# First weight's sums on VectorE, late loads of bias rows and rim, and score batches of two in layer 1 of a four-layer convolution sequence

## The chip, the cores and the metric

The kernel runs on one NeuronCore of one Trainium2 chip. The metric is device time in microseconds (us) of one execution, and the number to compare is the median of several runs. The engines are named as in the profile: PE is TensorE (matmuls), PEld its weight loads, DVE is VectorE, ACT is ScalarE, POOL is GpSimd, SP is SyncE, which here only issues DMAs.

## The reference

The input `x` is float32, 8 images of 512 channels of 32 by 32 pixels (S = 1024 positions). Four layers follow one another, cut here to what matters:

```python
# layer 0: group norm, eight-head attention over positions, three tanh steps, projection, residual
h = group_norm(x); q, k, v = split(qkv_w @ h + qkv_b)
h = softmax(q.T @ k / 8) @ v                    # per head, 64 channels each
for _ in range(3): h = h + 0.1 * tanh(inl_w @ h + inl_b)
x = x + proj_w @ h + proj_b
# layer 1: one attention with 64 channels for queries and keys, 512 for values, no scaling
q, k, v = Wq @ x + bq, Wk @ x + bk, Wv @ x + bv
x = softmax(q.T @ k) applied to v + x
# layer 2: add a bias per channel, 12-tap upsampling by 2, leaky relu, 12-tap downsampling by 2
# layer 3: mixture of eight experts: 1x1, 3x3 and 1x1 convolutions whose weights are mixed per image
```

Everything is float32.

## The kernel before

**Stages.** The batch loop runs over the eight images `b`. For each it does `layer0`, `layer1` and `layer2`; layer 3 follows for all images at the end. `x_next` of the next image is loaded and its norm statistics are taken while the present image is worked on.

**Products in seven steps.** The 512 by 512 products (q, k, v, the tanh steps, the projection, and layer 1's values) are done by a Strassen-like scheme on quarters, in the generator `product`. Each `next()` issues one of its seven steps: P1 and C11 accumulate in two banks "A" of the PSUM pool `ps_mm`; U2, U3, C21 in banks "X" and C22, C12 in banks "Y" of the pool `ps_sc`. The steps need sums of quarters of both operands: `quarter_sums` makes the data's sums on DVE (tiles named `T_...`, eight instructions), and for the first image `weight_sums` makes the weights' on POOL (parts 3 to 6 of the weight tile; part 2 is minus a22) and stores them in DRAM, from where later images load them. The weight tile's parts are used in the order A11 (P1), A12 (C11), S2 (U2), S3 (U3), S1 (C22), -A22 (C21), S4 (C12). P1 and C11 need no sums at all.

**Order of work.** Except where `manual_schedule` is written (layer 0's attention), a planner orders each engine's instructions: it follows program order where it can and takes a later instruction that is ready, by its own estimate, when an earlier one is not. All engines execute their own queue in order. A tile from a pool with n buffers waits until the n-th tile before it is released.

**Start.** SP issues the loads of `x` of image 0, of the quarters of the q, k and v weights, and of the q and k weights of layer 1 (`w_qk`). POOL issues the small constants, the bias rows `v_row`, `row_bias`, `bias2` (each broadcast to 128 partitions), and four writes of a zero tile `rim0` to the rims of the two DRAM scratch images `ypad`. DVE takes the statistics (L286), the norm factors (L295 to L308), then makes `h` (L314, four instructions of 128x1024) and the sums of `h`. POOL makes the sums of the q weights (L362 to L366), then those of k and v. The argument `held` of `weight_sums` puts a one-element copy ahead, into the sum's own place, so that the sums of k and v start only after the sums of `h`.

**Layer 1.** `quarter_sums` of `x`; a projection with 128 columns for q and k together (`qk`, L322) into the two banks of the pool `ps_tp`, copied out by DVE and ACT; then the steps of the value product and the scores are interleaved. `scores(t)` does one of eight tiles: two matmuls (r = 0 and 1) that use 64 rows of the array each and so run beside each other (L271), two banks for the results, from `ps_tp` where t is even and from `ps_mm` where it is odd, and two exponentials on ACT (L767). `totals(0)` sums the exponentials of the first half over the partitions with four one-column matmuls (L782) into one bank of `ps_tp`, and DVE takes the reciprocal (L786). Each of the two pools has two banks. After the last step the transposes of `x` (L808) and the product of the weights with the values (L905) follow. The order is given by

```python
        for _ in range(2):
            next(values)
        for steps in ((0,), (1, 2), (3, 4), (5, 6), (7,)):
            for t in steps:
                scores(t)
            next(values)
            if 4 in steps:
                totals(0)
```

**A second copy.** If a bound is exceeded the whole sequence would be run again with `shifted=True`; that copy is in the program and isn't run on these inputs.

Of the kernel before, what the change touches and what calls it, by code (L numbers as in the profile page):

```python
# [17 lines left out]
P = 128  # L18
B, C, H, W = 8, 512, 32, 32
S = H * W  # L20
# [33 lines left out]
def tile_sequence(ctx: ExitStack, tc: tile.TileContext, a: dict, out: bass.AP, shifted: bool):  # L54
# [12 lines left out]
    def big_tile(name, shape):  # L67
        return big.tile(shape, F32, tag="big", name=name)
# [5 lines left out]
    def tmp(name, n=HALF):  # L74
        if n == HALF:
            return work.tile([P, n], F32, tag="half", name=name, bufs=2)
        return work.tile([P, n], F32, tag="tmp", name=name, bufs=6)
# [37 lines left out]
    nc.vector.memset(seen_sums, 0.0)  # L115

    v_row = const.tile([P, C], F32, name="v_row")
    nc.gpsimd.dma_start(v_row, a["v_b"].partition_broadcast(P))
    qk1_b = const.tile([P, 1], F32, name="qk1_b")
    nc.gpsimd.dma_start(qk1_b[0:HD, :], a["bq"])  # L120
    nc.gpsimd.dma_start(qk1_b[HD:P, :], a["bk"])
# [1 line left out]

    row_bias = const.tile([P, C], F32, name="row_bias")
    bias2 = tmp("bias2")
    nc.gpsimd.dma_start(row_bias, a["bv"].partition_broadcast(P))
    nc.gpsimd.dma_start(bias2, a["bias"].partition_broadcast(P))
    nc.vector.tensor_add(row_bias, row_bias, bias2)

    up_op = const.tile([P, UR * UC], F32, name="up_op")  # L130
    up_left_op = const.tile([P, UR * UC], F32, name="up_left_op")
# [106 lines left out]


    rim0 = tmp("rim0")  # L240
    nc.vector.memset(rim0, 0.0)
    for t in ypad:
        nc.gpsimd.dma_start(t[0 : 3 * W], rim0[0 : 3 * W])
        nc.gpsimd.dma_start(t[(H + 3) * W :], rim0[0 : 2 * W])


    pooled = const.tile([P, CC, B], F32, name="pooled")
# [63 lines left out]
    def group_norm(b, x, mul, add):  # L311
        h = big_tile(f"h_{b}", [P, CC, S])
        for cc in range(CC):
            nc.vector.tensor_scalar(  # L314
                h[:, cc, :], x[:, cc, :], mul[:, cc : cc + 1], add[:, cc : cc + 1],
                ALU.mult, ALU.add,
            )
        return h
# [19 lines left out]
    def weight(key, b):  # L338
        if not b:
            return weight_sums(key, *weight_quarters(key, tmp(f"raw_{key}", S)))  # L340
        t = wpool.tile([P, len(PARTS), 2, QR], F32, tag="w", name=f"w_{key}_{b}", bufs=3)
        nc.sync.dma_start(t, stored[key])
        return t
# [14 lines left out]
    def weight_sums(key, t, a21, a22, held=None):  # L358
        if held is not None:

            nc.gpsimd.tensor_copy(t[:, 3, 0, 0:1], held)
        nc.gpsimd.tensor_add(t[:, 3], a21, a22)  # L362
        nc.gpsimd.tensor_sub(t[:, 4], t[:, 3], t[:, 0])
        nc.gpsimd.tensor_sub(t[:, 5], t[:, 0], a21)
        nc.gpsimd.tensor_sub(t[:, 6], t[:, 1], t[:, 4])
        nc.gpsimd.tensor_scalar(t[:, 2], a22, -1.0, None, ALU.mult)  # L366
        nc.gpsimd.dma_start(stored[key], t)
        return t

    def quarter_sums(name, src, ccs=(0, 1), into=None):  # L370


        t = into
        if t is None:
            made = big_tile(f"T_{name}", [P, 8, HALF])
            at = ((0, 1), (7, 2), (6, 3), (5, 4))
            t = [[made[:, i, :] for i in pair] for pair in at]
        for cc in ccs:
            b11, b12 = src[:, cc, 0:HALF], src[:, cc, HALF:S]
            b21, b22 = src[:, cc + 2, 0:HALF], src[:, cc + 2, HALF:S]  # L380
            nc.vector.tensor_sub(t[0][cc], b12, b11)
            nc.vector.tensor_sub(t[1][cc], b22, t[0][cc])
            nc.vector.tensor_sub(t[2][cc], b22, b12)
            nc.vector.tensor_sub(t[3][cc], t[1][cc], b21)
        return t
# [39 lines left out]
    def all_of(gen):  # L425
        for _ in gen:
            pass
# [140 lines left out]

    def layer0(b, x, norm, w):
        h = group_norm(b, x, *norm)  # L570
        t = quarter_sums(f"h_{b}", h)
        if b == 0:
            for key in "kv":
                w[key] = weight_sums(key, *held[key], t[3][1][:, 0:1])
        q = big_tile(f"q_{b}", [P, CC, S])
        k = big_tile(f"k_{b}", [P, CC, S])
        v = big_tile(f"v_{b}", [P, SC, C])
        all_of(product(f"q_{b}", w["q"], h, t, channels(f"q_{b}", q, qkv_b[:, 0:CC])))
        w["inl"] = weight("inl", b)
        all_of(product(f"k_{b}", w["k"], h, t, channels(f"k_{b}", k, qkv_b[:, CC : 2 * CC])))  # L580
        w["proj"] = weight("proj", b)
# [22 lines left out]
        def scores(t):  # L604
            g, jc = divmod(t, SC)
            oc, sh = groups[g]
            pair = ps_sc.tile([P, S], F32, tag="scores", name=f"scores_{b}_{t}")
            ps = [pair[:, ts(r, HALF)] for r in range(2)]
            for r in range(2):
                for c in range(2):  # L610
                    nc.tensor.matmul(  # L611
                        ps[r][rows[c]],
                        k[rows[r], oc, jc * P + c * HD : jc * P + c * HD + HD],
                        q[rows[r], oc, ts(sh, HALF)],
                        start=True, stop=(shifts is None),
                    )
            if shifts is not None:
                for r in range(2):
                    nc.tensor.matmul(
                        ps[r], ones[HD * r : HD * r + 1, :],  # L620
                        shifts[HD * r : HD * r + 1, oc, ts(sh, HALF)],
                        start=False, stop=True, skip_group_check=True,
                    )
            e = tmp(f"e_{b}_{t}", S)
            nc.scalar.activation(e, pair, AF.Exp, scale=HD ** -0.5)  # L625
            exps[t] = e
            if jc == 1:
                accs[g] = sums(f"acc_{b}_{g}")
                nc.vector.tensor_add(accs[g], exps[t - 1], e)  # L629
            elif 1 < jc < SC - 1:  # L630
                nc.vector.tensor_add(accs[g], accs[g], e)  # L631
            elif jc == SC - 1:
                nc.vector.scalar_tensor_tensor(
                    accs[g], accs[g], 1.0, e, ALU.mult, ALU.add,
                    accum_out=seen_sums[:, b, g : g + 1],
                )
# [84 lines left out]
    def layer1(b, x, w, midway):  # L721
# [3 lines left out]

        rows = [slice(HD * r, HD * r + HD) for r in range(2)]
        t_x = quarter_sums(f"x_{b}", x)
        for sh in range(2):
            ps = bank(ps_tp, name=f"qk1_{b}_{sh}")
            project(ps, w["qk1"], 0, x, sh)  # L730
            keys = ps[HD:P, :].rearrange("d (p r j) -> d p r j", r=2, j=P)
            for r in range(2):
                dst = k[rows[r], 2 * sh : 2 * sh + 2, :]
                if r == 0:
                    nc.vector.tensor_scalar_add(q[rows[r], ts(sh, HALF)], ps[0:HD, :], qk1_b[0:HD, :])
                    nc.vector.tensor_scalar_add(dst, keys[:, :, r, :], qk1_b[HD:P, :])
                else:
                    nc.scalar.activation(
                        q[rows[r], ts(sh, HALF)], ps[0:HD, :], AF.Identity, bias=qk1_b[0:HD, :]
                    )  # L740
                    nc.scalar.activation(
                        dst, keys[:, :, r, :], AF.Identity, bias=qk1_b[HD:P, :]
                    )
        shift = None
        if shifted:
# [3 lines left out]
                [qk[rows[r], S : S + HALF] for r in range(2)],  # L749
                [shift[HD * r : HD * r + 1, :] for r in range(2)],  # L750
            )
        v = big_tile(f"v1_{b}", [P, SC, C])
        eT = [big_tile(f"eT_{b}_{sh}", [P, SC, HALF]) for sh in range(2)]
        inv = small.tile([P, SC], F32, tag="inv1", bufs=2, name=f"inv1_{b}")
        accs = {}
# [31 lines left out]
            nc.gpsimd.tensor_add(seen, seen, both)  # L787
            nc.gpsimd.tensor_add(seen[:, 0:4], seen[:, 0:4], inv[:, at])

        values = product(f"v1_{b}", w["v1"], x, t_x, positions(f"v1_{b}", v), rows=True)  # L790
        for _ in range(2):
            next(values)
        for steps in ((0,), (1, 2), (3, 4), (5, 6), (7,)):
            for t in steps:
                scores(t)
            next(values)
            if 4 in steps:
                totals(0)
        all_of(values)
        if b + 1 < B:  # L800
# [235 lines left out]
        return z  # L1036

    with tc.tile_pool(name=f"weights_{run}", bufs=1) as wpool:
        w = {"q": weight("q", 0)}
        raw = big_tile("raw_kv", [P, 2, S])  # L1040
        held = {key: weight_quarters(key, raw[:, i, :]) for i, key in enumerate("kv")}
        w["qk1"] = wpool.tile([P, CC, P], F32, name="w_qk1")
        for i, key in enumerate(("q1_wT", "k1_wT")):
            nc.sync.dma_start(
                w["qk1"][:, :, ts(i, HD)], a[key].rearrange("(cc p) o -> p cc o", p=P)
            )

        norm = norm_factors(0, channel_stats(0, x_next))
        for b in range(B):
            x, last = x_next, b + 1 == B  # L1050
            layer0(b, x, norm, w)
            if not last:
                x_next = load_x(b + 1)
            stats = []

            def midway():
                if not last:
                    stats.append(channel_stats(b + 1, x_next))

            halo = layer1(b, x, w, midway)  # L1060
            if not last:
                norm = norm_factors(b + 1, *stats)
                layer2(b, halo)
# [239 lines left out]
```

## Time and profile before

Three runs gave 3828.47, 3828.78 and 3829.96 us; the median is 3828.78 us. The execution that was profiled took 3826.37 us, of which 3824.6 us are the span from the first to the last instruction.

| | before |
|---|---|
| median of three runs | 3828.78 us |
| profiled execution, its span | 3826.37 us, 3824.6 us |
| mean granted TensorE clock | 0.997 |
| PE busy | 3764.8 us (98%) |
| DVE busy | 2572.6 us (67%) |
| ACT busy | 1202.9 us (31%) |
| POOL busy | 100.3 us (3%) |
| DMA | 248.67 MB, mean 65 GB/s |

In the timeline a row is: start in us, busy time in us, engine, line, operation, what it writes and reads, shape, count of instructions; in brackets, where the engine sat idle before it, how long and what ended that. A float32 matmul shows as two matmul records. In the chain of waits a row is start, length, and what the end of the kernel waited for in that stretch.

### The profile page before, as it was taken

The page shows a single profiled execution, that of the slowest core. Times are in us where ns is not written, and L with a number is a line of the kernel's source. Part 1 is how long each engine was busy: PE and PEld are TensorE (multiplying, and loading weights), DVE is VectorE, ACT ScalarE, POOL GpSimd, SP SyncE. Part 2 cuts the span into 40 slices and gives each one's busy share as a digit, 9 for nine tenths or more (in the row PEclk, how much of TensorE's full clock was granted, in tenths as well). Part 3 has the DMA queues.
Part 4 walks back from the last instruction along what each step waited for, and adds up shares of the span by engine and source line. Part 5 has one row for each costly group of instructions (what it writes and reads, how often), then busy time and mean ns, then how long its engine had stood idle before and what let it go on. Part 6 is the DMA issues. An engine that isn't in the chain of part 4 may idle for free.

```text
span 3824.6 us, 50438 instructions
## 1 busy us (share of the span) xinstructions
PE 3764.8 (98%) x20838; PEld 1996.0 (52%) x20838; DVE 2572.6 (67%) x3887; ACT 1202.9 (31%) x1707; POOL 100.3 (3%) x118
## 2 busy tenths in 40 slices
PE   8999999999999999999999999999999999999999
PEld 4346653475435753466534754357534754347543
DVE  5877948664686648775586647765487656866885
ACT  0631226212442116312252124422162123521333
POOL 5000000000000000000000000000000000001000
PEclk9999999999999999999999999999999999999999
DMA  5002310123101310023101220023201131003432
GB/s 199 24 1 86 115 63 1 42 76 106 39 1 61 121 70 11 1 85 119 58 1 61 84 92 27 1 80 102 80 1 42 52 129 41 1 1 124 161 145 98
DMA packets 85841, 248.67 MB, mean 65 GB/s; under 512 B 10480, under 2 KB 33024, under 8 KB 78816
## 3 DMA queue, kind: packets, MB, share of 16 engines
q1 hardware_dynamic: 69712, 220.23, 16.2%
q10 hardware_dynamic: 13824, 12.59, 1.0%
q0 software_dynamic: 2064, 12.51, 0.9%
q8 instruction: 166, 2.72, 0.3%
q14 instruction: 75, 0.61, 0.1%
HBM read 185.40 MB, written 59.90 MB: 64 GB/s over the span
## 4 chain that ended last, share of the span: by engine, by line
PE 93%; DVE 4%; ACT 1%; DMA 1%; issue 0%; SPq 0%; ACTq 0%; DVEq 0%
PE scores L611 12%; PE av L647 12%; PE inl_X L417 6%; PE dn L995 5%; PE v_X L417 4%; PE inl_A L417 4%; PE inl_Y L417 4%; PE up L971 4%; PE av_X L905 3%; PE c L1209 3%; PE v_Y L417 3%; PE av_A L905 3%; PE av_Y L905 2%; PE v_A L417 2%; PE proj_X L417 2%; PE q_X L417 2%
## 5 line engine op out<-in xcount | busy, mean ns | idle before, releaser
L625 ACT ACTIVATE e<-scores 128x1024 f32<-128x1024 f32 x512 | 523.2, 1024 | 673.5 <-PE scores L611 624.8
L611 PE MATMUL scores<-q,k 64*64 64x512 f32 x4096 | 535.8, 593 | 3.6 <-DVE v L498 3.6
L647 PE MATMUL av<-e,v 64*64 64x512 f32 x4096 | 531.0, 589 | 0.0
L631 DVE TENSOR_TENSOR acc<-acc,e 128x1024 f32<-128x1024 f32 x320 | 389.5, 1217 | 38.5 <-ACT e L625 36.5
L611 PEld LDWEIGHTS scores<-q,k 64*64 64x64 f32 x4096 | 153.8, 133 | 297.6 <-issue 208.5
L647 PEld LDWEIGHTS av<-e,v 64*64 64x64 f32 x4096 | 161.3, 133 | 278.2 <-issue 275.2
L417 PE MATMUL inl_X<-T_hf,w_inl 128*128 128x512 f32 x576 | 262.9, 592 | 0.0
L955 DVE SCALAR_TENSOR_TENSOR up<-up,leak 128x512 f32<-128x512 f32 x264 | 173.5, 688 | 115.3 <-ACT leak L954 110.0
L954 ACT ACTIVATE leak<-up 128x512 f32<-128x512 f32 x264 | 149.5, 596 | 249.5 <-DVE up L955 127.7
L668 DVE RECIPROCAL inv<-av 128x256 f32<-128x256 f32 x128 | 223.0, 1747 | 0.0
L995 PEld LDWEIGHTS dn<-dn_op,up 128*64 128x64 f32 (+1 forms) x4096 | 193.2, 136 | 56.5 <-issue 28.8
L995 PE MATMUL dn<-dn_op,up 128*64 128x126 f32 (+5 forms) x4096 | 210.5, 255 | 8.8 <-DVE up L955 7.9
L971 PE MATMUL up<-halo,up_op 126*128 126x512 f32 (+1 forms) x384 | 183.7, 611 | 0.8 <-DVE up L955 0.6
L417 PEld LDWEIGHTS inl_X<-T_hf,w_inl 128*128 128x128 f32 x576 | 108.7, 190 | 138.6 <-issue 105.8
L417 PE MATMUL inl_A<-hf,w_inl 128*128 128x512 f32 x384 | 172.2, 594 | 0.0
L511 ACT ACTIVATE inl_U<-inl_U,inl_b 128x512 f32<-128x512 f32 x96 | 66.7, 718 | 307.6 <-DVE inl_U L526 307.6
L629 DVE TENSOR_TENSOR acc<-e,e 128x1024 f32<-128x1024 f32 x64 | 78.8, 1232 | 112.0 <-ACT e L625 112.0
L522 DVE TENSOR_TENSOR inl_U<-inl_X,inl_P 128x512 f32<-128x512 f32 x96 | 61.9, 687 | 121.7 <-PE inl_X L417 118.9
L1209 PE MATMUL c<-rim,mixed 128*128 128x512 f32 x288 | 124.9, 592 | 0.0
L417 PEld LDWEIGHTS inl_A<-hf,w_inl 128*128 128x128 f32 x384 | 72.2, 190 | 94.6 <-issue 90.4
L905 PE MATMUL av_X<-v,eT 128*128 128x256 f32 x512 | 118.8, 380 | 1.8 <-DVE av_W L884 1.0
L905 PE MATMUL av_A<-v,eT 128*128 128x256 f32 x512 | 119.1, 381 | 0.0
(304 smaller groups left out, 5561.1 us busy)
## 6 DMA issues: line engine op xcount, KB each, us to landing
halo<-ypad_u SPq DMA_DIRECT2D x128, 252.0 KB
halo<-ypad_u SPq DMA_DIRECT2D x128, 198.0 KB
w_v<-stored_u_v SPq DMA_DIRECT2D x14, 1792.0 KB
x<-in_x_dram SPq DMA_DIRECT2D x32, 512.0 KB
spill_u<-z SPq DMA_DIRECT2D x28, 512.0 KB
z<-spill_u SPq DMA_DIRECT2D x28, 512.0 KB
out_dram<-z SPq DMA_DIRECT2D x28, 512.0 KB
w_q<-stored_u_q SPq DMA_DIRECT2D x7, 1792.0 KB
```

Of the source, the lines that this page charges most:

```text
L417: nc.tensor.matmul(dst, lhs, rhs, start=(opens and s == 0 and cc == 0), stop=(cc == 1 and s == rows), skip_group_check=True,)
L611: nc.tensor.matmul(ps[r][rows[c]], k[rows[r], oc, jc * P + c * HD : jc * P + c * HD + HD], q[rows[r], oc, ts(sh, HALF)], start=True, stop= ...
L625: nc.scalar.activation(e, pair, AF.Exp, scale=HD ** -0.5)
L631: nc.vector.tensor_add(accs[g], accs[g], e)
L647: nc.tensor.matmul(avs[g][r][rows[c]], v[rows[r], jc, ts(2 * oc + c, HD)], e[rows[r], ts(c, HALF)], start=(jc == 0), stop=(jc == SC - 1),)
L668: nc.vector.reciprocal(copies[g][:, at], totals[g][:, at])
L905: nc.tensor.matmul(ps[:, ts(s, QR)], left[:, j, at : at + P], right[:, j, :], start=(what in ("P1", "U2", "W") and s == 0 and j == 0), sto ...
L954: nc.scalar.mul(t, ps, 0.2 * SQRT2)
L955: nc.vector.scalar_tensor_tensor(dst, ps, SQRT2, t, ALU.mult, ALU.max)
L971: nc.tensor.matmul(ps[i], op[0 : IR * n, :], halo.tile(t)[0 : IR * n, c + i, :], start=True, stop=True,)
L995: nc.tensor.matmul(rows[part, r0 - first : r1 + 1 - first, c0 : c1 + 1], up[t][0:k, c, ts(2 * cc + s, HD)], op[:, r0 - 4 * t + 3 : r1 + 4 ...
L1209: nc.tensor.matmul(banks[g].rearrange("p (h w) -> p h w", w=W), wt[:, at : at + P], h1[:, ky + 16 * g : ky + 16 * g + 16, kx : kx + W], st ...
```

## The change

The sums of the first weight (q, image 0) are made on DVE by `first_sums` and `first_rest`, one of them (part 2) on ACT, instead of by `weight_sums` on POOL: two of them before the sums of `h`, two after. `first_sums` is held until the last quarter of `h` is written. The sums of k and v stay on POOL, where now three one-element copies each, instead of one, hold them back. The loads of `v_row`, `row_bias` and `bias2` and the four writes of the rim move from POOL's queue to SP's, behind the loads of all first weights; the zero tile is set by POOL instead of DVE; the addition of `bias2` to `row_bias` moves behind image 0's q product.

In layer 1 the first step of the value product (P1) comes ahead of the projection of q and k, and the scores come in four batches of two behind three steps, instead of in batches of one, two, two, two, one behind two steps. `totals(0)` comes after the batch of t = 4 and 5 and step C21; before, it came after t = 3 and 4 and step C22.

In the copy with `shifted=True` the added term of layer 0's scores is done by four matmuls instead of two.

```diff
-    nc.gpsimd.dma_start(v_row, a["v_b"].partition_broadcast(P))
...
-    nc.gpsimd.dma_start(row_bias, a["bv"].partition_broadcast(P))
-    nc.gpsimd.dma_start(bias2, a["bias"].partition_broadcast(P))
-    nc.vector.tensor_add(row_bias, row_bias, bias2)
...
     rim0 = tmp("rim0")
-    nc.vector.memset(rim0, 0.0)
-    for t in ypad:
-        nc.gpsimd.dma_start(t[0 : 3 * W], rim0[0 : 3 * W])
-        nc.gpsimd.dma_start(t[(H + 3) * W :], rim0[0 : 2 * W])
+    nc.gpsimd.memset(rim0, 0.0)
+
+    def late_loads():
+        nc.sync.dma_start(v_row, a["v_b"].partition_broadcast(P))
+        nc.sync.dma_start(row_bias, a["bv"].partition_broadcast(P))
+        nc.sync.dma_start(bias2, a["bias"].partition_broadcast(P))
+        for t in ypad:
+            nc.sync.dma_start(t[0 : 3 * W], rim0[0 : 3 * W])
+            nc.sync.dma_start(t[(H + 3) * W :], rim0[0 : 2 * W])
...
     def weight_sums(key, t, a21, a22, held=None):
         if held is not None:
-            nc.gpsimd.tensor_copy(t[:, 3, 0, 0:1], held)
+            for i in (3, 5, 2):
+                nc.gpsimd.tensor_copy(t[:, i, 0, 0:1], held)
...
+    def first_sums(t, a21, a22, held):
+        nc.vector.tensor_copy(t[:, 3, 0, 0:1], held)
+        nc.vector.tensor_add(t[:, 3], a21, a22)
+        nc.vector.tensor_sub(t[:, 4], t[:, 3], t[:, 0])
+
+    def first_rest(t, a21, a22):
+        nc.vector.tensor_copy(t[:, 5, 0, 0:1], t[:, 4, 0, 0:1])
+        nc.vector.tensor_sub(t[:, 5], t[:, 0], a21)
+        nc.scalar.mul(t[:, 2], a22, -1.0)
+        nc.vector.tensor_sub(t[:, 6], t[:, 1], t[:, 4])
+        nc.gpsimd.dma_start(stored["q"], t)
+        return t
...
     def layer0(b, x, norm, w):
         h = group_norm(b, x, *norm)
+        if b == 0:
+            first_sums(*held["q"], h[:, CC - 1, 0:1])
         t = quarter_sums(f"h_{b}", h)
         if b == 0:
+            w["q"] = first_rest(*held["q"])
             for key in "kv":
                 w[key] = weight_sums(key, *held[key], t[3][1][:, 0:1])
...
         all_of(product(f"q_{b}", w["q"], h, t, channels(f"q_{b}", q, qkv_b[:, 0:CC])))
+        if b == 0:
+            nc.vector.tensor_add(row_bias, row_bias, bias2)
...
         t_x = quarter_sums(f"x_{b}", x)
+        v = big_tile(f"v1_{b}", [P, SC, C])
+        values = product(f"v1_{b}", w["v1"], x, t_x, positions(f"v1_{b}", v), rows=True)
+        next(values)
         for sh in range(2):
             ps = bank(ps_tp, name=f"qk1_{b}_{sh}")
             project(ps, w["qk1"], 0, x, sh)
...
         for _ in range(2):
             next(values)
-        for steps in ((0,), (1, 2), (3, 4), (5, 6), (7,)):
-            for t in steps:
+        for first in range(0, SC, 2):
+            for t in (first, first + 1):
                 scores(t)
             next(values)
-            if 4 in steps:
+            if first == 4:
                 totals(0)
...
-        w = {"q": weight("q", 0)}
+        w = {}
+        held = {"q": weight_quarters("q", tmp("raw_q", S))}
         raw = big_tile("raw_kv", [P, 2, S])
-        held = {key: weight_quarters(key, raw[:, i, :]) for i, key in enumerate("kv")}
+        for i, key in enumerate("kv"):
+            held[key] = weight_quarters(key, raw[:, i, :])
...
+        late_loads()
```

## The prediction

> **What bounds the kernel now.** The page first: busy time and the chain that ended last.
>
> ```profile
> PE 3764.8 (98%) x20838; PEld 1996.0 (52%) x20838; DVE 2572.6 (67%) x3887; ACT 1202.9 (31%) x1707; POOL 100.3 (3%) x118
> ...
> PE 93%; DVE 4%; ACT 1%; DMA 1%; issue 0%; SPq 0%; ACTq 0%; DVEq 0%
> ```
>
> PE sets the end nearly everywhere, so an edit counts only where it removes an idle PE or PE time itself. Where PE is idle I looked up in PE's waits and, in the two stages that the change touches, in the timeline. The start, all engines:
>
> ```profile
> 13.56 0.48 DVE L241 MEMSET rim<- 128x512 f32 x1
> ...
> 15.17 9.57 PE L417 MATMUL q_A<-h,w_q 128*128 128x512 f32 x16 [2.37 <-DVE h L314]
> ...
> 17.01 1.67 POOL L362 TENSOR_TENSOR w_q<-raw_q 128x512 f32<-128x512 f32 x1
> ...
> 17.48 1.75 DVE L128 TENSOR_TENSOR row_bias<-row_bias,bias 128x512 f32<-128x512 f32 x1
> ...
> 20.82 1.75 DVE L381 TENSOR_TENSOR T_h<-h 128x512 f32<-128x512 f32 x1
> ...
> 26.06 1.10 PE L417 MATMUL q_X<-T_h,w_q 128*128 128x512 f32 x2 [1.32 <-DVE T_h L382]
> ...
> 28.11 0.68 DVE L382 TENSOR_TENSOR T_h<-h,T_h 128x512 f32<-128x512 f32 x1
> ...
> 28.85 2.84 PE L417 MATMUL q_X<-T_h,w_q 128*128 128x512 f32 x6 [1.69 <-DVE T_h L382]
> ...
> 45.26 7.03 PE L417 MATMUL k_A<-h,w_k 128*128 128x512 f32 x16
> ```
>
> To be seen: DVE needs 1.75 us for a sum of two SBUF operands while POOL computes (17.01 to 26.99) and 0.68 us when POOL is not computing; PE waits twice for those sums. Layer 1 of image 0, PE alone (the other seven images show the same lengths, shifted):
>
> ```profile
> 317.68 5.34 PE L417 MATMUL v_A<-w_v,x 128*128 128x256 f32 x24
> 323.27 1.99 PE L417 MATMUL v_A<-w_v,x 128*128 128x256 f32 x8 [0.25 <-ACT v_P L481]
> 325.19 1.13 PE L271 MATMUL scores<-qk 64*128 64x512 f32 x4
> 326.25 3.72 PE L417 MATMUL v_X<-w_v,T_x 128*128 128x256 f32 x16
> 329.90 1.99 PE L271 MATMUL scores<-qk 64*128 64x512 f32 x8
> ```
>
> And where `totals(0)` stands, all engines:
>
> ```profile
> 340.94 0.95 PE L782 MATMUL total<-ones,acc 128*128 128x1 f32 x8
> ...
> 341.14 1.29 DVE L498 TENSOR_TENSOR v<-v_Y,v_U 128x512 f32<-128x512 f32 x2 [1.45 <-PE v_Y L417]
> 341.82 1.99 PE L271 MATMUL scores<-qk 64*128 64x512 f32 x8
> ...
> 342.35 0.17 DVE L786 RECIPROCAL inv<-total 128x4 f32<-128x4 f32 x1
> ```
>
> The reciprocal stands on DVE behind the two additions of the step before and ends 0.70 us after the scores have started. That costs nothing now: t = 5, whose banks are free, goes first.
>
> **Start, q's wait.** Records of q_A are 0.59 us long at a pitch of 0.43 (weight loads at 20.72, 21.15, 21.58), so the next could follow 0.16 before the row's end: 24.74 - 0.16 = 24.58. Forty records remain, 40 x 0.43 = 17.2, so k could start at 41.8; it starts at 45.26. The two waits cost 3.5 us. After the change DVE makes h (four at a pitch of 0.72, from the rows at 14.30 and 15.03 in a narrow window), S1 and S2 (0.61 pitch each), eight sums of h (4.9), S3 and S4. From h's start at 14.3 less 0.8 (below): h to 16.5, S1 and S2 to 17.8, the sixth sum of h (the last that U2 needs, as now ordered) to 21.4, all to 22.6, the rest to 23.9. PE would reach U2 at 24.58 - 0.8 = 23.8. Slack 2.4 us, so the 3.5 us go whole. What is late next is PE's own rate. The cover goes only if POOL computes beside DVE: with 1.75 us for eight of these it would be 16.5 + 8 x 1.75 = 30.5, and the gain is lost. POOL's remaining sums (k, v) are held until the last sum of h, and its rim writes leave.
>
> S3 and S4 can meet POOL's k sums: two times 1.75 from 22.6, ready at 26.1 against U3 at 23.8 + 3.4 = 27.2. The Trainium skill, "SBUF — State Buffer", "Who interferes with whom", speaks against putting them there: a VectorE instruction with two SBUF inputs and a GpSimd one that reads SBUF exclude each other for the whole instruction. By that rule each could wait out one POOL sum (1.26 us alone, in the row of w_v at 33.05) and S4 would end at 22.6 + 2 x (1.26 + 0.68) = 26.5, an estimate; the sum is the same.
>
> **Start, ahead of h.** The zero tile's memset (0.48 us) stands on DVE between two norm factors, and the last statistics waited 0.35 us for x (row at 9.19). The first goes to POOL, which has idle time there (1.29 us before 8.14). The second should go with the bias rows (256 KB each, first issued at 4.46) out of x's way: 5 to 10 us is DMA at 345 GB/s and 98% busy. About 0.8 us together; bounds 0.4 (x no earlier) and 0.9. The first records are 0.86 us apart until about 20.1, 4.9 us after the first, though the granted clock reads 1.00; I take 4.9 as a length that moves along. If the fast pitch came at a fixed time, half of the 0.8 would be lost, 0.4. The Trainium skill, "TensorE: Matmul & The Clock Gate", "Part 1", says the slow state ends with a busy window of 3.4 us on a free-running grid; by it the slow stretch would be anything from 3.4 to 6.8 us, an estimate, as much noise as gain.
>
> **Start, at nothing.** Seven more issues on SP, about 0.4 us each like w_qk's, put the inl weights' loads 3 us later (17.45 to 20.5); POOL reads them at 45.52. `v_row` is first needed at about 70, the rims at 396. The row_bias addition (0.68 to 1.75) falls into the q product, where DVE is busy 10.4 of 20 us. ACT's multiplication (about 0.6) is needed by step C21, some 10 us after U2. Two more guard copies for k and v cost POOL 4 x 0.17; k's sums end near 32, used from 48. The second copy does not run. Start in all: -3.5 - 0.8 = **-4.3 us**, once; bounds -4.5 and -3.5.
>
> **Layer 1, removed.** (a) P1 now waits on ACT behind the copies of q and k: 24 records at 0.2155 from 317.68 end at 322.85, the next starts at 323.27: 0.42 us. With P1 ahead of q and k, ACT has copied it long before C11. (b) Two batches of one take 2 x 1.06 (325.19 to 326.25), one of two 1.92 (329.90 to 331.82): 0.20 less. A value step between batches takes 3.65 (326.25 to 329.90), without them 3.45 (the chain's v_X row in layer 0): another 0.20. Sum 0.82 us an image, 8 x 0.82 = **-6.6 us**. q and k are copied out within 4.9 us of their last matmul (317.7 to 322.6); C11 and U2 cover 6.9.
>
> **Layer 1, added.** After `totals(0)` the next scores are t = 6, in the pool whose second bank holds the totals. Its second matmul must wait for the reciprocal; t = 5, which covers that now, has gone. Relative to the totals' start, scores start at 0.88 and the reciprocal ends at 1.58, whether the step before is C22 or C21 (two additions either way). A weight load follows a DVE end by about 0.06, so r = 1 starts at 1.64 instead of 0.88: 0.76 us, and r = 0 and t = 7 stand behind it in PE's queue. 8 x 0.76 = **+6.1 us**. Lower bound 0, if the planner puts t = 7 ahead whole; upper bound 0.86 (one t alone) if it splits the pair so that the halves no longer run together. I take 0.76, the row as it stands. The batch's two exponentials more at the end (2.06 instead of 1.08) lie under C12's 3.65.
>
> **Sum.** -4.3 - 6.6 + 6.1 = -4.8 us on the profiled 3826.37 (span 3824.6, 1.8 outside). The profiled run is 2.4 below the median of 3828.78; the same difference on the median gives **3824.0 us**. A measurement here can tell about 0.2%, 7.7 us, from no change, so this case is "within".
>
> **Rivals.** A: no new wait, -4.3 - 6.6 = -10.9, 3817.9. For it: the planner takes what is ready, as its two qk matmuls amid the projection show. Against: t = 6 has one free bank, so it comes first, and t = 7 then only halves a pair.
>
> B: the start doesn't gain (POOL still beside DVE, or h's quarter sums before S2): -0.8 - 6.6 + 6.1, -1.3, 3827.5. For it: the planner ordered T_h and w_q as it liked. Against: the guards.
>
> C, slower: on DVE the sums of layer 1's last product (L856, two of 0.6, running right after C21's additions at 348.70 today) get ahead of the reciprocal, and with them an addition of exponentials (1.13). The wait becomes 0.76 + 1.2 = 2.0, or 3.1: -4.3 - 6.6 + 8 x 2.0 = +5.1, 3833.9, or +13.9, 3842.7. It decides from 1.36 us of wait (10.9 / 8). Against: today the reciprocal comes right after the additions.
>
> Beside these, PE's two long waits (6.47 us at 419.69 behind DVE, followed by a clock of 0.50; 5.62 at 3524) may shift by 2 us if the planner's order does; this is in every range.
>
> **How the numbers follow.** Main case 0.58 (3820 to 3828), A 0.22 (3816 to 3820), B 0.08, C 0.12. Over 0.2% faster (below 3821.1): nine tenths of A and a sixth of the main case, 0.30. Slower (above 3836.4): the longer form of C, two thirds of it, 0.08. Within: 0.62. The range 3816 to 3832 leaves out the lower edge of A and most of C.
>
> **What would show it.** q_X without a wait after q_A and k_A near 41; sums of h at 0.68; h at 13.5. In layer 1 no wait for v_P, four score batches, and between the totals and t = 6 a wait for DVE's reciprocal of some 0.7 us, eight times. Without that wait, A; with more DVE work ahead of L786, C. A PE wait elsewhere than these makes it wrong.

## Result and profile after

The changed kernel took 3831.87 us (median of 22 runs, 3824.95 to 3846.33), the kernel before 3828.41 us on the same chip (22 runs, 3825.99 to 3831.52). The ratio is 1.0013, 95% interval 1.0008 to 1.0019: slower by 0.13% (by the two medians alone, 0.09%). That lies inside the forecast's range and within its 0.2%, but 7.9 us above the forecast, and the kernel became slower where it was to become 4.8 us faster. The profiled execution took 3831.41 us, with a span of 3829.6 us (before: 3824.6).

The page after, busy time and the chain that ended last:

```profile
PE 3773.7 (99%) x20838; PEld 2004.4 (52%) x20838; DVE 2568.8 (67%) x3892; ACT 1206.7 (32%) x1708; POOL 88.2 (2%) x111
...
PE 94%; DVE 3%; DMA 1%; ACT 1%; issue 0%; SPq 0%; ACTq 0%; DVEq 0%
```

PE is 8.9 us longer busy with the same number of instructions. So the time was lost in matmuls that took longer, or that look longer because something stands between them. The timeline of the start, all engines:

```profile
13.73 2.98 DVE L315 TENSOR_SCALAR h<-x,gmul,gadd 128x1024 f32<-128x1024 f32 x4
14.60 8.93 PE L432 MATMUL q_A<-h,w_q 128*128 128x512 f32 x16 [2.01 <-DVE h L315]
...
17.90 0.68 DVE L374 TENSOR_TENSOR w_q<-raw_q 128x512 f32<-128x512 f32 x1
...
23.37 3.60 PE L432 MATMUL q_X<-T_h,w_q 128*128 128x512 f32 x8
...
40.54 5.74 PE L432 MATMUL k_A<-h,w_k 128*128 128x512 f32 x13
```

q_X follows q_A without a wait, the sums take 0.68 us, and k starts at 40.54 instead of 45.26. The start did what was forecast; what of the 4.72 us is the change's own is worked out below. Layer 1 of image 0, PE alone:

```profile
316.31 3.62 PE L432 MATMUL v_A<-w_v,x 128*128 128x256 f32 x16
319.77 3.62 PE L432 MATMUL v_X<-w_v,T_x 128*128 128x256 f32 x16
323.31 1.99 PE L272 MATMUL scores<-qk 64*128 64x512 f32 x8
325.23 3.72 PE L432 MATMUL v_X<-w_v,T_x 128*128 128x256 f32 x16
...
339.93 0.95 PE L805 MATMUL total<-ones,acc 128*128 128x1 f32 x8
340.80 3.79 PE L272 MATMUL scores<-qk 64*128 64x512 f32 x8
344.52 2.64 PE L432 MATMUL v_Y<-w_v,x 128*128 128x256 f32 x11
```

The wait for `v_P` is gone. But the batch behind the totals takes from 340.80 to 344.52, 3.72 us, where the batch at 323.31 takes 1.92 (to 325.23) with the same eight records. No idle time of PE stands at it. The same stretch with the other engines:

```profile
340.80 0.29 PEld L272 LDWEIGHTS scores<-qk 64*128 64x128 f32 x2
...
341.33 0.17 DVE L809 RECIPROCAL inv<-total 128x4 f32<-128x4 f32 x1
...
341.96 0.60 ACT L790 ACTIVATE eT<-scores 128x512 f32<-128x512 f32 x1 [4.29 <-PE scores L272]
...
342.61 0.29 PEld L272 LDWEIGHTS scores<-qk 64*128 64x128 f32 x2 [0.66 <-ACT eT L790]
342.82 0.60 ACT L790 ACTIVATE eT<-scores 128x512 f32<-128x512 f32 x1 [0.26 <-PE scores L272]
```

The wait stands in the row of the weight load: at 342.61 it waits for ACT's first exponential, which ends at 341.96 + 0.60 = 342.56. The matmul held there is read as t = 6, r = 1: it has been given the bank that r = 0 of the same t wrote, so it can't start until that has been read (experiment 5, where it stands second in the queue, shows the same wait). Meanwhile r = 0 of t = 7, on the same half of the array as r = 0 of t = 6, fills PE, and the two r = 1 follow on the other half. Eight records then stand one behind the other (8 x 0.43 + 0.28 = 3.72) instead of in four pairs (4 x 0.43 + 0.20 = 1.92). The reciprocal, at 341.33 to 341.50, is not what it waits for. Of PE's waits the changed kernel shows none at these scores, and of the weight loads' waits exactly eight, one an image:

```profile
PEld scores L272 <- issue: 27.2, 104, 0.5
...
PEld scores L272 <- ACT eT L790: 5.3, 8, 0.7
```

(A row is: total idle in us, how often, mean in us.) In the kernel before the second row doesn't exist. In image 6 the stretch cost more. Windows from 3001 us, with PE's busy time first and the granted clock in the third column from the end:

```profile
3001.00:3008.30 7.30, 7.30 (x32) 5.14 (x31) 4.38 (x7) 2.75 (x6) 0.50 (x1) 1.00 0.00 0
3008.30:3015.20 6.90, 6.90 (x14) 4.04 (x14) 3.66 (x4) 1.30 (x3) 1.26 (x1) 0.51 0.01 2
3015.20:3022.00 6.80, 6.80 (x45) 5.98 (x44) 5.40 (x8) 0.00 (x0) 0.00 (x0) 1.00 0.66 228
```

The clock was granted at half for 6.8 us, beginning amid this batch, and the image lost another 3.33 us. Half-clock stretches are in the trace of before too (10.24 us from 416.06, 6.83 us from 3522.19), but those two begin in PE's long waits in layer 2. Here PE's records leave no gap.

### The profile page after: what moved, and what is told of

Read it like the earlier page. It is cut to its first block, busy times and chain, and to the rows that moved or that the text cites. A ratio compares the mean times of both kernels' runs of the same rounds, so it can differ in the third digit from the quotient of the medians.

```text
span 3829.6 us, 50461 instructions
## 1 busy us (share of the span) xinstructions
PE 3773.7 (99%) x20838; PEld 2004.4 (52%) x20838; DVE 2568.8 (67%) x3892; ACT 1206.7 (32%) x1708; POOL 88.2 (2%) x111
## 4 chain that ended last, share of the span: by engine, by line
PE 94%; DVE 3%; DMA 1%; ACT 1%; issue 0%; SPq 0%; ACTq 0%; DVEq 0%
PE scores L631 12%; PE av L668 11%; PE inl_X L432 6%; PE dn L1017 5%; PE v_X L432 4%; PE inl_A L432 4%; PE inl_Y L432 4%; PE up L993 4%; PE av_X L927 4%; PE c L1234 3%; PE v_Y L432 3%; PE av_A L927 3%; PE v_A L432 3%; PE av_Y L927 2%; PE q_X L432 2%; PE proj_X L432 2%
```

## Experiments

"k minus h" is the time from the first `h` to the first record of k_A. Layer 1 is compared per image, from the first scores of layer 0's attention to the first transpose (L808 before). Intervals are of the ratio to the kernel before.

**1. The start alone, layer 1 as before.**

```diff
-        for first in range(0, SC, 2):
-            for t in (first, first + 1):
+        for steps in ((0,), (1, 2), (3, 4), (5, 6), (7,)):
+            for t in steps:
...
-            if first == 4:
+            if 4 in steps:
```
(and P1 back behind q and k)

> The changed start, layer 1 as in the kernel before. Theory M (the loss is all in layer 1's last score batch, where the halves of t = 6 and t = 7 no longer run in pairs): the changed kernel's k_A starts at 40.54 instead of 45.26, so 4.7 us less than before, about 3823.7, and nothing else moves; the clock of every run stays at 0.997 as before. Rival S (the start's gain is given back later, at image 0's wait for DVE or by another clock period, so layer 1 isn't the cause): within 1.5 us of before, or slower.

Measured: 3825.23 us against 3827.94, ratio 0.9990 (0.9981 to 0.9999). A gain of 2.7 us, the forecast's 4.3 within its interval. k minus h is 27.30, before 30.96.

**2. Layer 1 alone, the start as before.** The reverse of 1.

> The start as before, layer 1 changed. Theory M: eight times 0.9 us more up to the transposes, half of that given back in the product that follows, and in some runs a period of half clock more: 4 to 12 us slower than before, with runs that spread over 10 us and clocks down to 0.993; the totals are followed by scores that take 3.7 us instead of 1.9. Rival S: layer 1 costs nothing by itself, within 2 us of before, with a narrow spread.

Measured: 3839.43 us against 3827.94, ratio 1.0028 (1.0017 to 1.0039). The loss is layer 1's. In each of the eight images the last batch takes 3.72 us. The two halves of the change don't add up: -2.7 and +11.5 make +8.8, the whole change +3.5. The runs of 2 and of the whole change spread over 8 and 21 us, with mean clocks of 0.9951 and 0.9953; so the clock doesn't tell them apart. In the trace of 2 some 1.7 us went by a half-clock stretch of 3.41 us in the start (from 28.48, amid image 0's q product), which neither the kernel before nor the whole change has there; what the rest of the difference is stays open.

**3. The changed kernel with the last batch in the order (7, 6).**

```diff
-            for t in (first, first + 1):
+            for t in (first, first + 1) if first < 6 else (7, 6):
```

> The changed kernel, with t = 7 ahead of t = 6 in the last batch, nothing else. The banks of t = 7 are free at once, and t = 6 meets the reciprocal when it is done. Theory M: the batch takes 1.9 us again, 1.8 us less in each image: 8 x 1.8 = 14 less than the changed kernel, 3814 to 3818, and the spread is narrow again with clocks of 0.997. Rival N (the planner's order doesn't matter; t = 6 waits for the bank in any order, as I had assumed, 0.76 us): 3822 to 3826. Rival S: no change, 3828 to 3833.

Measured: 3819.39 us, ratio 0.9977 (0.9968 to 0.9986). That is 1.4 us above theory M's range and below that of N; what decides is the batch, which takes 1.92 us with no wait behind it. Each image's layer 1 is 0.92 us shorter than before; the stage behind it, from the first transpose to the first av_X, is 0.25 us longer (19.01, before 18.76). t = 7 has two free banks, and by its end the banks of t = 6 are free.

**4. P1 ahead of q and k, the five batches of before.**

```diff
-        for _ in range(2):
-            next(values)
-        for first in range(0, SC, 2):
-            for t in (first, first + 1):
+        next(values)
+        for steps in ((0,), (1, 2), (3, 4), (5, 6), (7,)):
+            for t in steps:
...
-            if first == 4:
+            if 4 in steps:
```

> The changed start and P1 ahead of q and k, but the batches of scores as before (one, two, two, two, one; the totals after t = 4). Tells the two parts of layer 1 apart. Theory M: 4.7 from the start and 8 x 0.42 from the wait for P1's copy, 8.1 less than before, about 3820.3, narrow spread. If P1 ahead is what costs (its seven steps then end one step earlier and the last scores stand alone): no faster than the start alone, 3823 or more.

Measured: 3820.81 us, ratio 0.9982 (0.9973 to 0.9991); 0.51 us an image. So of the 0.92 of experiment 3, 0.51 are P1 and 0.41 the batch saved.

**5. The changed kernel with PE held to the written order in the last batch.**

```diff
-            for t in (first, first + 1):
-                scores(t)
-            next(values)
+            if first < 6:
...
+            else:
+                with tc.manual_schedule(engines={mybir.EngineType.PE}):
+                    for t in (first, first + 1):
+                        scores(t)
+                    next(values)
```

> The changed kernel with TensorE held to the written order in the last batch and the step behind it: r = 0 and r = 1 of t = 6, then of t = 7, then C12. Theory M (the bank): t = 6's second matmul has been given the bank of its first, so it waits for that one's exponential. From the changed kernel's rows that ends at 342.56, 1.76 us after the scores' start; behind it the second matmul of t = 6 and the first of t = 7 fill a pair, and the last runs alone: about 3.7 us from the scores' start to C12 as in the changed kernel, so 3831.9 with 3826 to 3837. Theory N (the written order is all that was lost): both pairs are whole and only the reciprocal's 0.76 us stands in between, 1.92 + 0.76 = 2.7 us, 8 us less over eight images and less of the half clock, 3820 to 3825.

Measured: 3838.67 us, ratio 1.0029 (1.0018 to 1.0041): not the 3820 to 3825 of theory N, and above theory M's 3837. PE's timeline of image 0:

```profile
340.83 0.95 PE L805 MATMUL total<-ones,acc 128*128 128x1 f32 x8
341.71 1.12 PE L272 MATMUL scores<-qk 64*128 64x512 f32 x2
343.52 2.83 PE L272 MATMUL scores<-qk 64*128 64x512 f32 x6 [0.69 <-ACT eT L790]
346.28 4.21 PE L432 MATMUL v_Y<-w_v,x 128*128 128x256 f32 x9
```

With nothing to run meanwhile the wait becomes visible as PE's: the third record starts 1.81 us behind the first, as in the changed kernel. At full clock (five images) the batch takes 3.72 us here too. Images 0, 1 and 5 fell to half the clock amid it, 3.33 us each. Without these 10.0 us the profiled run would have taken 3827.3 us for 3837.29, which is what the changed kernel takes at a clock of 0.997. The clocks of all runs are 0.993 to 0.995. So the planner's order cost nothing: it had filled the wait.

**6. The totals of layer 1 in a bank of the other pool, order (6, 7) kept.**

```diff
-            ps = bank(ps_tp, f"total1_{b}_{sh}")
+            ps = bank(ps_mm, f"total1_{b}_{sh}")
```

> The changed kernel with the totals of layer 1 in a bank of the other PSUM pool (ps_mm for ps_tp); the order of the batches stays (6, 7). Theory M (the bank): t = 6 finds both banks of its pool free, its matmuls stand as a pair right behind the totals, t = 7 follows as a pair and has the reciprocal behind it by then; the last batch takes 1.9 to 2.0 us instead of 3.7, and the time is that of the kernel with the batch (7, 6): 3819.4, with 3816 to 3824. Theory N (what helped there was that t = 7's exponentials come first, not the bank): the batch keeps over 3 us, 3828 to 3833.

Measured: 3816.45 us, ratio 0.9968 (0.9956 to 0.9980), the fastest of all. PE's and ACT's rows in image 0:

```profile
339.90 0.95 PE L805 MATMUL total<-ones,acc 128*128 128x1 f32 x8
...
340.78 1.99 PE L272 MATMUL scores<-qk 64*128 64x512 f32 x8
...
341.94 2.06 ACT L790 ACTIVATE eT<-scores 128x512 f32<-128x512 f32 x4 [4.29 <-PE scores L272]
...
342.69 2.64 PE L432 MATMUL v_Y<-w_v,x 128*128 128x256 f32 x11
```

One line, and the four exponentials run without a gap. Beside experiment 3, `totals(1)` starts earlier as well (1.12 us behind the first transpose of image 0, there 9.87), and the transposes' stage is 0.48 us an image shorter (18.53 us, there 19.01).

**7. The pairs of t = 2 and 3 written r = 0, r = 0, r = 1, r = 1, far from the totals** (on the kernel of experiment 3; `half(t, r, ...)` is one matmul of `scores`).

```diff
+            if first == 2 and not shifted:
+                with tc.manual_schedule(engines={mybir.EngineType.PE}):
+                    both = [banks(t) for t in (2, 3)]
+                    for r in range(2):
+                        for t in (2, 3):
+                            half(t, r, both[t - 2])
...
```

> The kernel with the last batch in the order (7, 6), and in the batch of t = 2 and 3, far from the totals, the matmuls written r = 0, r = 0, r = 1, r = 1 and held to that. No wait is added. Theory M (the price is that of two broken pairs): the batch takes 3.7 us instead of 1.92, 8 x 1.8 = 14.4 us, of which up to 0.7 us an image may come back where VectorE's backlog is smaller: 9 to 14 us above 3819.4, 3828 to 3834 at an unchanged clock. On the clock, theory H (a poorly filled array alone brings the half clock): granted clocks down to 0.994 and single runs to 3845; theory T (it takes the one-column totals as well): clocks of 0.996 to 0.997 in nearly all runs and a spread of under 9 us.

Measured: 3821.15 us (0.9978, 0.9969 to 0.9987), 1.8 us above experiment 3, with clocks of 0.996 and 0.997: theory M's price was wrong, so H and T weren't tried. The batch stays at 1.92 us (328.82 to 330.74). PE's weight loads, and ACT's exponentials of this batch:

```profile
328.82 0.31 PEld L272 LDWEIGHTS scores<-qk 64*128 64x128 f32 x4 [0.33 <-issue]
329.35 0.20 PEld L272 LDWEIGHTS scores<-qk 64*128 64x128 f32 x2 [0.23 <-issue]
329.78 0.20 PEld L272 LDWEIGHTS scores<-qk 64*128 64x128 f32 x2 [0.23 <-issue]
330.74 0.30 PEld L432 LDWEIGHTS v_Y<-w_v,T_x 128*128 128x128 f32 x2 [0.76 <-issue]
...
329.98 0.60 ACT L805 ACTIVATE eT<-scores 128x512 f32<-128x512 f32 x1 [3.50 <-PE scores L272]
330.84 1.58 ACT L805 ACTIVATE eT<-scores 128x512 f32<-128x512 f32 x3 [0.26 <-PE scores L272]
```

Both halves are loaded at 328.82, although the other half's first matmul stands third in the queue. That the queue has the written order is read from two places: ACT's second exponential waits until 330.84, for t = 3, although both first matmuls end near 329.95; and of the first two weight loads only one waits on a count of ACT, as it must if the load of t = 3, r = 0 stands between them and has waited for a later count already (experiment 3 shows such a wait at all four). So "all engines execute their own queue in order", as said of the kernel before, doesn't hold for PE's two halves here. Where nothing waits, the order within the batch does not break the pairs. This took "the order" out of the theory and left the bank.

**8. Late loads, but the first weight's sums on POOL again** (on the kernel of experiment 3; the hold on the sums of k and v is one copy each, as before).

```diff
-        held = {"q": weight_quarters("q", tmp("raw_q", S))}
+        held = {}
+        w["q"] = weight_sums("q", *weight_quarters("q", tmp("raw_q", S)))
...
```

> The kernel with the last batch in the order (7, 6), with the late loads, but the first weight's sums on GpSimd again as before the change. Theory M (VectorE's sums are what the start gains): q waits twice for the sums of h again, k starts some 31 us after the first h instead of 27.3, 3.3 to 3.7 us; 3819.4 + 3.5 = 3822.9, with 3820 to 3826. Theory L (the late loads alone quicken the sums): k starts 27 to 28 us after the first h, and the time stays at 3819.4. On the other 0.8 us: if the late loads bring x earlier, h starts at or below 14.3 here; if its landing only varies from run to run, anywhere from 13.7 to 15.4.

Measured: 3824.54 us (0.9990, 0.9981 to 0.9999), 5.1 us above experiment 3 and within theory M's range. k minus h is 29.83, between the two theories, and the sums beside POOL are slow again:

```profile
20.33 2.32 DVE L395 TENSOR_TENSOR T_h<-h 128x512 f32<-128x512 f32 x1
22.57 3.22 DVE L397 TENSOR_TENSOR T_h<-h 128x512 f32<-128x512 f32 x1
25.71 1.09 DVE L396 TENSOR_TENSOR T_h<-h,T_h 128x512 f32<-128x512 f32 x1
26.73 0.68 DVE L395 TENSOR_TENSOR T_h<-h 128x512 f32<-128x512 f32 x1
```

k minus h flatters this kernel, because `h` itself is late. POOL's sums now begin at 12.14, and beside them the norm factor of L308 takes 1.18 us, in the changed kernel 0.16. From the end of the last statistics to k it takes 34.52 us, before 34.54, in the changed kernel 30.02 (without the half of PE's slow first stretch that is lost, worked out in the next section: 31.5, 32.1 and 28.2). The greater part of the start's gain is the DVE sums, not the loads.

**9 and 10. More matmuls in the last batch, on one half of the array or on both** (on the kernel of experiment 6). The matmuls of t = 6 are done three times over; the second kernel has `(0, 1)` for `(0,)`.

```diff
+            if t == 6:
+                for _ in range(2):
+                    for r in (0,):
+                        nc.tensor.matmul(
+                            ps[r], k[rows[r], p, :], q[rows[r], at], start=True, stop=True
+                        )
```

> The kernel with the totals in the other pool, and in the last batch the first matmul of t = 6 (64 of the 128 rows) done three times over, each overwriting the one before: 4 records more on one half of the array, no wait, the result the same. The half's lane then takes 4 x 0.86 + 0.28 = 3.7 us, as long as the last batch of the changed kernel: 8 x 1.8 = 14.4 us more than 3816.45, of which up to 0.7 us an image may come back behind it, 3825 to 3831 at an unchanged clock. Theory H (it is the poorly filled array, not the wait, that brings the half clock): granted clocks of 0.994 to 0.996 in several runs, single runs to 3840, and a median 3 to 8 us above the kernel with the same filler on both halves. Theory W (it takes the other thing, a matmul held by a wait): clocks of 0.996 to 0.997 and no more than 2 us between the two.

> The same filler on both halves of the array: the matmuls of t = 6 done three times over as pairs. The last batch takes 3.7 us here too, 3825 to 3831. Under theory H its clock stays at 0.996 to 0.997 and its spread under 9 us; under theory W it is like the kernel with the filler on one half.

Measured: 3829.50 us (1.0002, 0.9993 to 1.0010) on one half, 3828.05 us (0.9999, 0.9990 to 1.0008) on both; the batch takes 3.63 us in both, and every run's clock is 0.996 or 0.997. The filler on one half brings no clock below 0.996. At 0.996 are 5 of its 11 runs, with the filler on both halves 4. This leans to theory W, but doesn't settle it: here the other half had matmuls for half of the stretch, where in the changed kernel only one half ever ran.

**11. Both cures together: totals in the other pool and order (7, 6).** The edits of 3 and 6.

> The mirror of the changed kernel: totals in the other pool, and the last batch in the order (7, 6), so that again the t that comes first shares its pool with the totals. Theory M (the bank): t = 7's second matmul gets the bank of its first and waits for that one's exponential, 1.81 us behind the start, the last batch takes 3.72 us again, and both cures together lose what each alone brings: 3826 to 3834, clocks below 0.996 in some runs. Rival (each cure brings something of its own): 3812 to 3817.

Measured: 3831.40 us (1.0009, 1.0000 to 1.0018; 3825.26 to 3843.24, clocks 0.993 to 0.997). The loss is back in full, in PE's timeline of image 0 with the very length of the changed kernel:

```profile
341.36 0.95 PE L805 MATMUL total<-ones,acc 128*128 128x1 f32 x8
342.24 3.79 PE L272 MATMUL scores<-qk 64*128 64x512 f32 x8
345.96 1.35 PE L432 MATMUL v_Y<-w_v,x 128*128 128x256 f32 x5
```

Image 3 of this trace fell to half the clock amid the batch as well (6.83 us from 1682.20, 3.33 us lost). Neither the pool nor the order matters by itself, only whether the t that comes first behind the totals shares its pool with them.

## Why the prediction was wrong, step by step

**Start, q's wait (-3.5): right.** k minus h was 30.96 us before, 32.44 in experiment 2, 29.83 in experiment 8, and 26.59 to 27.88 in the ten profiles of kernels with the changed start: 3.1 to 4.4 us less than before. Part of that is not the change's. q_A's first records follow one another by 0.85 us, the later ones by 0.43, and the slow stretch isn't the fixed 4.9 us that the prediction took it for: 4.95 us before, 3.66 in the changed kernel's profile, 3.22 to 5.81 in the other nine. Half of it is lost time. Without that half, k minus h is 26.81 - 3.66 / 2 = 24.98 us in the changed kernel, 24.97 or 24.98 in the other nine, and 30.96 - 4.95 / 2 = 28.48 before: 3.50 less, the forecast's term to the digit. So the second guard copies, the issues on SP and the `row_bias` addition cost PE nothing that shows there. The k of the profiled run came 4.72 us earlier: 3.50 by the sums, 0.57 by an earlier `h`, and 0.65 by a shorter slow stretch, which is luck.

**Start, ahead of h (-0.8): half of it is there.** The term has two parts. The memset's is steady: from the last row of the statistics to `h` it takes 3.79 and 3.80 us in the two profiles with the zero tile on DVE, 3.42 or 3.43 in the ten of the changed start, 0.37 less. That of `x` isn't: that row starts at 10.51 and 10.54 in the two profiles with the early loads, and anywhere from 10.13 to 12.12 with the late ones, where the statistics waited for a later part of `x` by up to 1.88 us. `x` lands that differently from run to run. In the profiled run `h` started 0.57 us earlier (13.73 for 14.30). As a gain that can be counted on the term is 0.4, the prediction's lower bound.

**Layer 1, removed (-0.82 an image): right.** Experiments 3 and 6 gave -0.92 in every image, experiment 4 split it into 0.51 and 0.41 (forecast 0.42 and 0.40). The stage of the transposes behind it, which the prediction held unchanged, gave 0.25 of it back in experiment 3 and saved another 0.23 in experiment 6.

**Layer 1, added (+0.76 an image): this step failed.** The text said that t = 6's "second matmul must wait for the reciprocal", because the pool's other bank held the totals. It was given the bank of t = 6's first matmul and waited for that one's exponential (the rule that a tile waits for the n-th tile before it, taken in the written order, names the totals' bank; why the pool handed out the other one no run shows): 1.81 us behind the scores' start, made up of 0.96 (two records), 0.20 to the exponential, 0.60 of exponential and 0.05 to the load. The upper bound of 0.86 "if it splits the pair" took one t alone; both were. The step measured +1.80 an image. Of that 0.43 came back in the transposes' stage, where DVE is less behind (18.33 us from the first transpose to av_X, before 18.76). So layer 1 came to -0.92 + 1.80 - 0.43 = +0.45 an image instead of -0.06, 8 x 0.51 = 4.1 us in all.

**What no step had: the half clock behind that wait.** The runs of the changed kernel with a clock of 0.997 took 3824.95 to 3827.91 us, the median 3831.87. So at most some 5 us of it go with the lower clock, at 3.33 us a half-clock stretch; in the kernel before, too, the lowest run lies 2.4 us below the median. All four kernels with the wait have runs at 0.995 or below, none of the eight others tried here has one below 0.996, nor has the kernel before in the runs beside them.

The traces show where it strikes. The granted clock changes on a grid: in experiment 5 it falls at 344.51, 416.19, 801.89 and 2573.41 us, and these lie 21, 113 and 519 times 3.413 us apart, so the grid can be carried on to every image of a trace. In the four traces of kernels with the wait, five batches of 32 fell to half the clock. In these five a grid point stands 0.01 to 0.27 us behind the first record of the totals, and the clock falls at the next one; in the other 27 none stands between 0 and 0.40 us behind it. In the nine traces without the wait eleven grid points stand there (0.01 to 0.28 us), one of them with the filler on both halves, and the clock held in all. So it took both: the wait, and a window of 3.41 us that began with the totals and held only most of them (0.6 us or more of 0.88) and the first 2.5 to 2.8 us of the waiting batch. With the grid at random that is 8 x 0.3 / 3.41 = 0.7 stretches a run, 2.3 us, an estimate. In the trace of experiment 9 no grid point stands so (the nearest is at 0.66), so for the filler on one half there are only its runs' clocks.

With the two put in, 3824.0 + 4.1 + 2.3 to 5 is 3830 to 3833, against 3831.87 measured. Where in this the true share of the clock lies stays open.

**The rivals.** A, no new wait, was wrong as a forecast of this kernel (3817.9), but experiments 3 and 6 are that case: 3819.39 and 3816.45. B was wrong: the start gained. C had the right sign and nearly the right time (3833.9), by another mechanism: no sum got ahead of the reciprocal. "A PE wait elsewhere than these makes it wrong" was to be the sign; it was a wait that PE's rows didn't show at all.

The Trainium skill, "TensorE: Matmul & The Clock Gate", "Part 1", says that the clock is set by the activity in free-running windows of 3413 ns and halves after an idle one. The stretches measured here, 6.83 and 10.24 us, are two and three such windows. That the array must be idle for it is not what image 6 shows: no gap in PE's records (whose ends the profile models) and the clock at 0.51. What in that window counts as too little activity stays open.

## What to carry to other kernels

Before counting on what a matmul will wait for, work out every bank that the pool can hand it, not only the one that comes free first; the costlier one here was the exponential of its own pair, 1.81 us against the reciprocal's 0.76. Where half-array matmuls can run meanwhile, such a wait hides in PE's busy time: compare the length of the row with that of its like elsewhere, and read the releaser in the weight loads' rows. A one-column sum that borrows a bank belongs in the pool which the next scores don't use first; that one line made this change a gain of 0.32% over the kernel before (ratio 0.9968, 0.9956 to 0.9980).

## Not expected of the hardware

Two matmuls on different halves of the array started 0.01 us apart though another on the first half stood between them in the queue (experiment 7). And a stretch in which PE has records throughout can be followed by half the clock: 0.51 for 6.8 us in image 6 of the changed kernel and in image 3 of experiment 11. It depends on where the clock's own grid of 3.413 us falls: to within 0.3 us behind the totals' start in all five batches that fell, and in none of the 27 others with the same wait.
